# DMA queue in program order, and the two norms' statistics at other places, in a fused window-attention and Fourier kernel

## The chip, the core and the metric

The kernel runs on one core of one Trainium2 chip. The time is device microseconds (us) from the launch to the end of the program; the median of repeated runs is compared. A core has a matrix engine (TensorE, "PE" in the profile, with its weight loads as "PEld"), a vector engine (VectorE, "DVE"), an activation engine (ScalarE, "ACT"), a general engine (GpSimd, "POOL") and SyncE ("SP"), which here does nothing but issue DMA transfers. Each engine works through its own list of instructions in order; semaphores make one engine wait for another.

## What is computed

The input has 32 images of 56 x 56 pixels with 128 channels, float32. Layer 0 is a shifted-window attention, layer 1 a Fourier mixing with a feed-forward part; each has a group norm (32 groups of 4 channels) in front and a residual around it. Cut to what matters:

```python
def reference(x, ...):
    x = x + _L0_conv_ref(_gn(x), rpb_table, w_qkv, w_proj, b_proj)
    x = x + _L1_conv_ref(_gn(x), w0, w1, W1, b1, W2, b2)
    return x
# _gn: mean and variance of each group of 4 channels over the whole image
# _L0: roll by 3, cut into 7x7 windows, qkv, softmax(q k / sqrt(32) + bias + mask) v, projection
# _L1: DCT along the width, mix 32 modes with w0, inverse DCT; the same along the height with w1;
#      sum; then relu(h @ W1 + b1) @ W2 + b2
```

So layer 1's norm of an image can be finished only when the attention of all its rows is done, and layer 0's norm only when the whole image has been read.

## The kernel before: the parts that matter

An image is treated as 8 rows of windows (`NWR` = 8). The outer loop counts cycles: in cycle 8b + i the scores of row i of image b are made. A row's steps are spread over several cycles, so several rows are under way at once: three cycles later its values are multiplied and projected, and in the cycle after that its statistics for the second norm are taken. Layer 1 of image b follows 11 cycles behind: its stage c is cycle - 11 - 8b, and c goes from 0 to 15. Stage 0 of one image and stage 8 of the image before fall into the same cycle, the one in which row 3 of a later image has its scores.

The statistics of the second norm. `part` holds, for every row, the sums and the sums of squares; `fourier_stats` adds the 8 rows up, and a matmul with a constant matrix takes the mean over the partitions:

```python
def attn_sums(im, i):                      # one row, two halves
    nc.vector.tensor_reduce(im.part[:, 0, :, i], piece..., axis=AX.XY, op=ALU.add)
    yield
    nc.scalar.activation(sq, piece, AF.Square)
    nc.vector.tensor_reduce(im.part[:, 1, :, i], sq..., axis=AX.XY, op=ALU.add)
    yield

def fourier_stats(im):
    nc.vector.tensor_reduce(tot..., im.part..., axis=AX.X, op=ALU.add)
    yield
    pg = attn_bank()
    halved(pg[:, : C // 2], gmean, tot...)             # two matmuls, 64 output rows each
    ...                                                # own, ms, nm2, ve on VectorE
    nc.gpsimd.tensor_tensor(rstd, ve, mhalf, ALU.pow)  # the reciprocal root, on GpSimd
    nc.vector.scalar_tensor_tensor(out=shift, in0=ms[:, 0:1], scalar=-SQRT_S, in1=rstd, ...)
    yield
```

The first norm of the next image is a generator too. Its first part (on VectorE and GpSimd) ends with `rstd`; the second makes `nb` on VectorE and the scaled weights `im.w` on ScalarE; the third is a matmul of `nb`:

```python
def image_norm(im):
    yield
    nc.vector.bn_aggr(...); ...                        # eleven small VectorE steps
    nc.gpsimd.tensor_tensor(rstd, ve, mhalf, ALU.pow)
    yield
    nc.vector.scalar_tensor_tensor(out=nb, in0=gm, scalar=-1.0, in1=rstd, ...)
    nc.scalar.mul(im.w, wqkv, rstd)
    yield
    pb = attn_bank()
    halved(pb[:, 0:1], wqkv[:, 2 * C :], nb)
    ...
```

The feed-forward part reads the residual `res` back from DRAM (`scr`), adds a bias on GpSimd, and adds the result on VectorE when it is done:

```python
def ff_in(im, g):
    res = work.tile([P, 4, C], F32, tag="res", name="res")          # two buffers
    nc.sync.dma_start(res[:, :k], scr_tok[t0 : t0 + k * P]...)
    nc.gpsimd.tensor_tensor(res..., res..., b2sb..., ALU.add)
    ...                                                              # first matmul, relu -> hid
def ff_out(im, g):
    ...                                                              # second matmul -> pf
    nc.vector.tensor_tensor(res..., pf..., res..., ALU.add)
    nc.sync.dma_start(out_tok[...], res...)
```

One cycle of the steady part, with the order in which the instructions are written down:

```python
def halves_first(cycle, norm):
    last, j = row(cycle - 4)
    if last:
        sums = attn_sums(last, j); next(sums)      # sums of the row before
    im, i = row(cycle)
    if im: attn_qk(im, i, False)                   # q, k of this row
    next(norm)                                     # image_norm, first part
    if last: next(sums)                            # sums of squares
    for im, c in fourier(cycle):
        if c == 0: im.stats = fourier_stats(im); next(im.stats)      # tot
    for im, c in fourier(cycle):
        if c in FF_AT: ff_in(im, FF_AT.index(c))   # FF_AT = (8, 9, 10, 12, 13, 14, 15)
    for im, c in fourier(cycle):
        if c == 0: next(im.stats)                  # matmul of tot, rstd, shift

# then: values of row - 3, scores of this row, modes_back (inverse DCT, its sum into xf is
# VectorE's where it is along the width), transposes; and at the end of the cycle
def halves_last(cycle, norm):
    im, i = row(cycle)
    if im: attn_v(im, i, cycle)
    if has_ff(cycle): half_columns(cycle)          # the DCT (transform) or the mixing
    half_columns(cycle, True)
    load_back(cycle + 1); next_begin(cycle); load_first(cycle)       # DMA loads
    if row(cycle)[0]: attn_exp(cycle); attn_divide(cycle)
    next(norm)                                     # image_norm, second part
    im, j = row(cycle - 3)
    if im: last_out(cycle); attn_project(im, j)    # ff_out; projection, row stored to scr
    next(norm)                                     # image_norm, third part
```

`transform` and `modes_back` share four PSUM banks (`pc`). The order is kept as written on TensorE, ScalarE, VectorE and GpSimd; the order of the transfers on SyncE is left to the scheduler of the framework:

```python
with tc.manual_schedule(engines={ET.PE, ET.Activation, ET.DVE, ET.Pool}):
```

The first 11 cycles, before layer 1 starts, have their own routine (`first_rows`); there the statistics of the attention rows are taken four cycles behind in one go.

Of the kernel before, what the change touches and what calls it, by code (L numbers as in the profile page):

```python
# [17 lines left out]
C = 128  # L18
# [6 lines left out]
NWR = S // WS  # L25
# [23 lines left out]
def swin_fourier_kernel(  # L49
# [58 lines left out]
    def halved(dst, lhsT, rhs, start=True, stop=True):  # L108

        for p in range(0, dst.shape[0], P // 2):  # L110
            ps = slice(p, min(p + P // 2, dst.shape[0]))
            nc.tensor.matmul(dst[ps], lhsT=lhsT[:, ps], rhs=rhs, start=start, stop=stop)  # L112
# [19 lines left out]
    def const_load(shape, src, name):  # L132
        t = const.tile(shape, F32, tag=name, name=name)
        (nc.scalar if name in FIRST else nc.sync).dma_start(t, src)
        return t
# [47 lines left out]
    bm = const.tile([P, 2, 2, NP, 2, WT], F32, tag="bm", name="bm")  # L183
    nc.gpsimd.memset(bm, 0.0)
    rpb_f = rpb.rearrange("p (t u) y x -> p t u (y x)", u=2)
    for r in range(2):
        for t in range(2):
            for half in range(2):
                rows = slice(half * JP, half * JP + WT)
                for k, p0, p1 in ((0, 0, NP - half), (1, NP - half, NP)):  # L190
                    for p in range(p0, p1):
                        nc.vector.tensor_tensor(
                            bm[rows, r, t, p],
                            rpb_f[rows, t],
                            mask_sb[rows, r, k].unsqueeze(1).to_broadcast([WT, 2, WT]),
                            ALU.add,
                        )

    dct_w = const_load([TC, 2 * NM], dct, "dct_w")
    dct_h = const.tile([TC, 2 * NM], F32, tag="dct_h", name="dct_h")  # L200
    for r in range(0, TC, S):
# [375 lines left out]
    def fourier_stats(im):  # L577
        tot = small.tile([TC, 2, C // 4], F32, tag="tot", name="tot")
        nc.vector.tensor_reduce(
            tot.rearrange("p k g -> p (k g)"),  # L580
            im.part.rearrange("p k g i -> p (k g) i"),
            axis=AX.X,
            op=ALU.add,
        )
        yield
        pg = attn_bank()

        halved(pg[:, : C // 2], gmean, tot.rearrange("p k g -> p (k g)"))
        own = small.tile([P, 2, C // 4], F32, tag="own", name="own", bufs=1)
        nc.vector.scalar_tensor_tensor(  # L590
            out=own,
            in0=pg[:, : C // 2].rearrange("p (k g) -> p k g", k=2),
            scalar=4.0,
            in1=gavg.rearrange("p (g c) -> p g c", c=4)[:, :, 0]
            .unsqueeze(1)
            .to_broadcast([P, 2, C // 4]),
            op0=ALU.mult,
            op1=ALU.mult,
        )
        ms = small.tile([P, 2], F32, tag="ms", name="ms")  # L600
        nc.vector.tensor_reduce(ms, own, axis=AX.X, op=ALU.add)
        nm2 = small.tile([P, 1], F32, tag="nm2", name="nm2")
        nc.vector.scalar_tensor_tensor(
            out=nm2, in0=ms[:, 0:1], scalar=-1.0, in1=ms[:, 0:1], op0=ALU.mult, op1=ALU.mult
        )
        ve = small.tile([P, 1], F32, tag="ve1", name="ve1")
        nc.vector.scalar_tensor_tensor(
            out=ve, in0=nm2, scalar=1e-5, in1=ms[:, 1:2], op0=ALU.add, op1=ALU.add
        )
        rstd = small.tile([P, 1], F32, tag="rstd1", name="rstd1")  # L610
        nc.gpsimd.tensor_tensor(rstd, ve, mhalf, ALU.pow)
        shift = small.tile([P, 1], F32, tag="shift", name="shift")
        nc.vector.scalar_tensor_tensor(
            out=shift, in0=ms[:, 0:1], scalar=-SQRT_S, in1=rstd, op0=ALU.mult, op1=ALU.mult
        )
        im.rstd, im.shift = rstd, shift
        im.zT, im.zscr = {}, {}
        yield
# [197 lines left out]
    def row(r):  # L816
        return (images[r // NWR], r % NWR) if 0 <= r < NB * NWR else (None, 0)
# [12 lines left out]
    def load_back(cycle):  # L830
        for im, c in fourier(cycle):
            for width, g in back_groups(c):
                load_modes(im, width, g)

    def load_first(cycle):
        for im, c in fourier(cycle):
            if c == 0:
                load_columns(im, 0)
                load_columns(im, 1)

    def halves_first(cycle, norm):
        last, j = row(cycle - 4)
        if last:
            sums = attn_sums(last, j)
            next(sums)
        im, i = row(cycle)
        if im:
            attn_qk(im, i, False)
        next(norm)
        if last:  # L850
            next(sums)
        for im, c in fourier(cycle):
            if c == 0:
                im.stats = fourier_stats(im)
                im.cols = {}
                next(im.stats)
        for im, c in fourier(cycle):
            if c in FF_AT:
                ff_in(im, FF_AT.index(c))
        for im, c in fourier(cycle):  # L860
            if c == 0:
                next(im.stats)
# [46 lines left out]
    def next_groups(cycle):  # L909
        b, i = divmod(cycle, NWR)  # L910
        if b + 1 < NB:
            for j in {5: (0, 2), 6: (4, 6)}.get(i, ()):
                image_groups(images[b + 1], j)

    def last_out(cycle):
# [4 lines left out]
    def halves_last(cycle, norm):  # L920
        im, i = row(cycle)
        if im:
            attn_v(im, i, cycle)
        if has_ff(cycle):
            half_columns(cycle)
        half_columns(cycle, True)
        load_back(cycle + 1)
        next_begin(cycle)
        load_first(cycle)
        if row(cycle)[0]:  # L930
            attn_exp(cycle)
            attn_divide(cycle)
        next(norm)
        im, j = row(cycle - 3)
        if im:
            last_out(cycle)
            attn_project(im, j)
        next(norm)
# [10 lines left out]
    def first_rows(cycle, norm):  # L949
        im, i = row(cycle)  # L950
        if im:
            attn_qk(im, i, True)
        if cycle:
            attn_exp(cycle - 1)
        im3, i3 = row(cycle - 3)
        if im3:
            attn_values(im3, i3, cycle - 3)
        im2, i2 = row(cycle - 2)
        if im2:
            attn_transpose(im2, i2, cycle - 2)  # L960
        if cycle:
            attn_divide(cycle - 1)
        if im:
            attn_scores(im, i, cycle)
            attn_max(cycle)
        if im3:
            attn_project(im3, i3)
        next(norm)
        last, j = row(cycle - 4)
        if last:  # L970
            for _ in attn_sums(last, j):
                pass
        if im:
            attn_v(im, i, cycle)
        if cycle < NWR // 2:
            image_bias(im, 2 * cycle)
        next(norm)
        next_begin(cycle)
        next_groups(cycle)
        if cycle == CONV_BEGIN - 1:  # L980
            attn_exp(cycle)
            attn_divide(cycle)
            last, j = row(cycle - 1)
            attn_transpose(last, j, cycle - 1)
        next(norm)

    def nothing():
        while True:
            yield

    ET = mybir.EngineType
    with tc.manual_schedule(engines={ET.PE, ET.Activation, ET.DVE, ET.Pool}):
        images[0] = image_begin(0)
        for i in range(0, NWR, 2):
            image_groups(images[0], i)
        for _ in image_norm(images[0]):
            pass
        norm = nothing()
        for cycle in range(NB * NWR + CONV_BEGIN + FF_AT[-1] - NWR + 1):
            if cycle < CONV_BEGIN:  # L1000
                first_rows(cycle, norm)
            else:
                halves_first(cycle, norm)
                if not row(cycle - 3)[0]:
                    half_columns(cycle)
                    half_columns(cycle, True)
                    load_first(cycle)
                    last_out(cycle)
                    quarters(cycle)
                    load_back(cycle + 1)  # L1010
                    continue
                if not has_ff(cycle):
                    half_columns(cycle)
                eighths(cycle)
                quarters(cycle)
                if row(cycle)[0] and cycle % 2:
                    attn_max(cycle)
                full(cycle)
                halves_last(cycle, norm)
            b, i = divmod(cycle, NWR)  # L1020
            norm = nothing()
            if i == NWR - 2 and b + 1 < NB:
                norm = image_norm(images[b + 1])
                next(norm)

# [61 lines left out]
```

## Time and profile before

Three runs took 3663.43, 3664.92 and 3668.95 us; the median is 3664.92. The profiled run spans 3662.0 us.

| engine | busy, us | share of the span | instructions |
|---|---|---|---|
| PE | 3574.7 | 98% | 72064 |
| PEld | 2832.1 | 77% | 72064 |
| DVE | 2216.2 | 61% | 4738 |
| ACT | 2147.2 | 59% | 4044 |
| POOL | 1368.1 | 37% | 1421 |

How to read it: an engine's busy time is the union of its instructions; what is left of the span is idle time, and the profile says for each idle stretch what ended it ("PE ... <- DVE nb" is time in which PE waited for the instruction on DVE that writes `nb`). A busy PE need not be at its peak: the ends of matmuls are modelled, and the clock may be halved. By stretches of 100 us, PE is busy 73.20 us in the first, 81.88 in the second, 96.47 in the third and 97.69 to 99.81 from then on to 3600 us; the mean granted clock is 0.95 in the first stretch, 0.90 in the second and 1.00 after it. The matmul of `tot` comes once per image: at 2222.8 us and at 3117.4 us, eight images apart, so an image takes 111.8 us. The DMA engines are busy for some 40% of the span.

### The profile page before, as it was taken

How to read it: one execution, taken by the hardware profiler on the slowest of the kernel's cores; microseconds unless marked ns; L12 is line 12 of the kernel's file. 1: busy time of each engine (PE TensorE's matmuls, PEld its weight loads, DVE VectorE, ACT ScalarE, POOL GpSimd, SP SyncE). 2: the span in 40 equal slices, each digit the busy share in tenths (PEclk: the TensorE clock that was granted, in tenths of full speed). 3: DMA queues.
4: the chain of work that ended last, by engine and by line, in shares of the span. 5: the costliest groups of instructions: out<-in, count | busy, mean ns of one | idle time of the engine just before them, and what ended most of it. 6: DMA issues, size and time to landing. Idle time of an engine off the chain costs nothing.

```text
span 3662.0 us, 161441 instructions
## 1 busy us (share of the span) xinstructions
PE 3574.7 (98%) x72064; PEld 2832.1 (77%) x72064; DVE 2216.2 (61%) x4738; ACT 2147.2 (59%) x4044; POOL 1368.1 (37%) x1421
## 2 busy tenths in 40 slices
PE   7899999999999999999999999999999999999999
PEld 5677777777787777787877877777778778777776
DVE  7666665666666666656666666666566666666641
ACT  5555566555556555566555566555655556565553
POOL 5333334333434333333334343334433343433321
PEclk9999999999999999999999999999999999999999
DMA  4333433444334444334443344443344433443343
GB/s 114 85 101 105 117 97 108 108 108 113 107 96 113 110 111 109 99 105 109 111 113 105 99 109 113 105 113 100 106 109 111 113 106 98 109 113 105 97 117 98
DMA packets 687349, 390.29 MB, mean 107 GB/s; under 512 B 39967, under 2 KB 657600, under 8 KB 686400
## 3 DMA queue, kind: packets, MB, share of 16 engines
q1 hardware_dynamic: 686045, 379.65, 38.1%
q8 instruction: 567, 9.29, 1.1%
q14 instruction: 126, 1.03, 0.1%
q10 hardware_dynamic: 611, 0.32, 0.0%
HBM read 218.29 MB, written 161.48 MB: 104 GB/s over the span
## 4 chain that ended last, share of the span: by engine, by line
PE 77%; DVE 15%; ACT 3%; POOL 3%; issue 2%; DMA 1%; SPq 0%; POOLq 0%; DVEq 0%; ACTq 0%
PE pc L112 30%; PE pa L112 12%; PE pc L640 6%; PE pa L406 5%; PE pc L674 5%; PE pa L428 5%; PE pa L472 5%; PE pa L497 4%; PE pc L713 3%; PE pa L273 3%; POOL a L447 2%; DVE sm L458 2%; DVE a L436 2%; DVE xf L724 2%; ACT a L453 2%
## 5 line engine op out<-in xcount | busy, mean ns | idle before, releaser
L447 POOL TENSOR_TENSOR a<-a,mx 128x784 f32<-128x784 f32 x256 | 389.3, 1521 | 1439.7 <-DVE mx L446 1247.8
L112 PE MATMUL pc<-wff,hid 128*64 128x128 f32 x12544 | 739.9, 273 | 1.3 <-ACT hid L758 1.0
L112 PE MATMUL pc<-xf,wff 128*64 128x512 f32 (+2 forms) x3584 | 718.4, 539 | 1.0 <-DVE xf L724 1.0
L112 PEld LDWEIGHTS pc<-wff,hid 128*64 128x64 f32 x12544 | 702.7, 137 | 7.4 <-ACT hid L758 4.6
L458 DVE TENSOR_REDUCE sm<-a 128x16 f32<-128x784 f32 x256 | 248.2, 970 | 693.8 <-ACT a L453 692.9
L461 POOL TENSOR_TENSOR a<-a,rs 128x784 f32<-128x784 f32 x256 | 389.0, 1520 | 568.8 <-DVE rs L460 491.0
L758 ACT ACTIVATE hid<-pc,b1sb 128x512 f32<-128x512 f32 (+2 forms) x896 | 526.7, 632 | 76.3 <-PE pc L112 74.2
L112 PEld LDWEIGHTS pc<-xf,wff 128*64 128x64 f32 x3584 | 286.6, 137 | 361.1 <-issue 257.5
L377 ACT ACTIVATE q<-pa,bqkv 128x392 f32<-128x392 f32 x256 | 150.4, 588 | 466.7 <-PE pa L112 460.9
L112 PE MATMUL pa<-xw,wn 128*64 128x392 f32 (+1 forms) x2048 | 393.3, 499 | 3.2 <-DVE a L436 3.2
L528 DVE TENSOR_SCALAR oT<-pa,bqkv 128x98 f32<-128x98 f32 (+2 forms) x768 | 171.1, 278 | 271.1 <-PE pa L497 271.1
L746 POOL TENSOR_TENSOR res<-res,b2sb 128x512 f32<-128x512 f32 (+2 forms) x256 | 264.0, 1037 | 113.6 <-DMA res<-scr 113.6
L453 ACT ACTIVATE a<-a 128x784 f32<-128x784 f32 x256 | 222.4, 869 | 112.2 <-POOL a L447 111.8
L413 ACT COPY v<-pa 128x512 f32<-128x512 f32 x256 | 150.9, 589 | 232.2 <-PE pa L406 232.2
L304 POOL TENSOR_TENSOR xl<-xl,bproj 112x512 f32<-112x512 f32 (+1 forms) x256 | 286.8, 1142 | 0.0
L406 PE MATMUL pa<-wn,xw 128*64 128x128 f32 x4096 | 283.1, 280 | 3.1 <-issue 3.1
L497 PEld LDWEIGHTS pa<-aT,v 49*32 49x32 f32 x16384 | 172.6, 105 | 139.6 <-issue 120.1
L436 DVE TENSOR_TENSOR a<-pa,bm 128x392 f32<-128x392 f32 x512 | 264.9, 560 | 24.1 <-PE pa L428 0.5
L480 ACT COPY aT<-pa 113x452 f32<-113x452 f32 x256 | 139.5, 545 | 206.1 <-PE pa L472 202.2
L406 PEld LDWEIGHTS pa<-wn,xw 128*64 128x64 f32 x4096 | 220.9, 137 | 37.7 <-issue 8.9
L394 DVE TENSOR_SCALAR k<-pa,heads,bqkv 128x392 f32<-128x392 f32 x245 | 167.2, 683 | 135.7 <-ACT k L386 133.1
L782 DVE TENSOR_TENSOR res<-pc,res 128x512 f32<-128x512 f32 (+3 forms) x257 | 140.2, 556 | 180.3 <-PE pc L112 146.5
(89 smaller groups left out, 5748.3 us busy)
## 6 DMA issues: line engine op xcount, KB each, us to landing
zscr<-z SPq DMA_DIRECT2D x512, 112.0 KB
htok<-scr SPq DMA_DIRECT2D x256, 196.0 KB
zT<-zscr SPq DMA_DIRECT2D x192, 256.0 KB
res<-scr SPq DMA_DIRECT2D x160, 256.0 KB
out_dram<-res SPq DMA_DIRECT2D x160, 256.0 KB
scr<-xl SPq DMA_DIRECT2D x128, 224.0 KB
xl<-in_x_dram SPq DMA_DIRECT2D x32, 784.0 KB
xl<-in_x_dram SPq DMA_DIRECT2D x32, 672.0 KB
```

The source lines that it names most:

```text
L112: nc.tensor.matmul(dst[ps], lhsT=lhsT[:, ps], rhs=rhs, start=start, stop=stop)
L304: nc.gpsimd.tensor_tensor(piece, piece, bproj.unsqueeze(1).to_broadcast([TC, e - a, C]), ALU.add)
L406: nc.tensor.matmul(pv[hs, j * C : (j + 1) * C], lhsT=im.xw[i][:, w * WT : w * WT + JP], rhs=im.w[:, 2 * C : 3 * C], start=True, stop=True,)
L436: nc.vector.tensor_tensor(a[:, 2 * hp : 2 * hp + 2, :, 0:WT].rearrange("p u w j -> p w u j"), ps[hp][:, :RT].rearrange("p (w u j) -> p w u ...
L447: nc.gpsimd.tensor_tensor(a3, a3, mx.unsqueeze(2).to_broadcast([P, 2 * NWR, WT]), ALU.subtract)
L453: nc.scalar.activation(a3, a3, AF.Exp)
L458: nc.vector.tensor_reduce(sm, a3, axis=AX.X, op=ALU.add)
L461: nc.gpsimd.tensor_tensor(a3, a3, rs.unsqueeze(2).to_broadcast([P, 2 * NWR, WT]), ALU.mult)
L497: nc.tensor.matmul(po4[u][h * HD : (h + 1) * HD, 2 * f + e], lhsT=v[ks, 2 * f + e, h * HD : (h + 1) * HD], rhs=im.aT[i][f][ks, h, e * JP : ...
L640: nc.tensor.matmul(py[hs, c * 2 * NM : (c + 1) * 2 * NM], lhsT=tok[:, c, hs], rhs=dct_sb, start=True, stop=True,)
L746: nc.gpsimd.tensor_tensor(res[:m, c0:c1], res[:m, c0:c1], b2sb[:m].unsqueeze(1).to_broadcast([m, c1 - c0, C]), ALU.add,)
L758: nc.scalar.activation(hf[:, :n], ph[:, :n], AF.Relu, bias=b1sb[:, f : f + 1])
```

## The change

It has five parts.

1. SyncE joins the engines whose order is kept as written, so that the DMA queue is filled in program order instead of the scheduler's.
2. The statistics of the second norm: the sum over rows (`tot`) is taken ahead of the last row, over 7 rows, at the start of the cycle; the last row's sums are added by a second matmul that accumulates into the same PSUM bank. At the first image the last row's sums are moved to the end of the cycle before.
3. The second part of the first norm (`nb` and the scaled weights) is put ahead of the exponential and the division instead of behind them.
4. The bias-and-mask table for the last row of an image (16 of 32 VectorE instructions) is made in cycle 1 instead of at the start.
5. Image 1's windows are cut and its norm is made one cycle earlier.

The idea of the parts 2 to 5 is to take VectorE and ScalarE work out of the way of matmuls that wait for it; part 1 makes the order of the transfers predictable.

```diff
@@ tables @@
-    for r in range(2):
+    def bias_and_mask(r):
         for t in range(2):
             for half in range(2):
... (the same 16 VectorE additions for each r)
+    bias_and_mask(0)
@@ fourier_stats @@
-            im.part.rearrange("p k g i -> p (k g) i"),
+            im.part.rearrange("p k g i -> p (k g) i")[:, :, : NWR - 1],
...
-        halved(pg[:, : C // 2], gmean, tot.rearrange("p k g -> p (k g)"))
+        rows = (tot, im.part[:, :, :, NWR - 1])
+        for k, t in enumerate(rows):
+            t = t.rearrange("p k g -> p (k g)")
+            halved(pg[:, : C // 2], gmean, t, start=(k == 0), stop=(k == 1))
@@ halves_first @@
-        last, j = row(cycle - 4)
-        if last:
-            sums = attn_sums(last, j)
-            next(sums)
-        im, i = row(cycle)
-        if im:
-            attn_qk(im, i, False)
-        next(norm)
-        if last:
-            next(sums)
         for im, c in fourier(cycle):
             if c == 0:
                 im.stats = fourier_stats(im)
                 im.cols = {}
                 next(im.stats)
+        last, j = row(cycle - 4)
+        sums = attn_sums(last, j) if last and cycle > CONV_BEGIN else nothing()
+        next(sums)
+        im, i = row(cycle)
+        if im:
+            attn_qk(im, i, False)
+        next(norm)
+        next(sums)
@@ next_groups @@
-            for j in {5: (0, 2), 6: (4, 6)}.get(i, ()):
+            for j in {(4 if b == 0 else 5): (0, 2), (5 if b == 0 else 6): (4, 6)}.get(i, ()):
@@ halves_last @@
+        next(norm)
         if row(cycle)[0]:
             attn_exp(cycle)
             attn_divide(cycle)
-        next(norm)
@@ first_rows @@
+        if cycle == 1:
+            bias_and_mask(1)
...
         if cycle == CONV_BEGIN - 1:
             attn_exp(cycle)
             attn_divide(cycle)
+            for _ in attn_sums(im3, i3):
+                pass
@@ main loop @@
-    with tc.manual_schedule(engines={ET.PE, ET.Activation, ET.DVE, ET.Pool}):
+    with tc.manual_schedule(engines={ET.PE, ET.Activation, ET.DVE, ET.Pool, ET.SP}):
...
-            if i == NWR - 2 and b + 1 < NB:
+            if i == (NWR - 2 if b else NWR - 3) and b + 1 < NB:
                 norm = image_norm(images[b + 1])
                 next(norm)
```

More of the change, by code (lines that the diff above doesn't have):

```diff
@@ L833, in load_back, with nothing @@
                 load_modes(im, width, g)
+    def nothing():
+        while True:
+            yield
     def load_first(cycle):
@@ L985, in first_rows @@
         next(norm)
-    def nothing():
-        while True:
-            yield
     ET = mybir.EngineType
-    with tc.manual_schedule(engines={ET.PE, ET.Activation, ET.DVE, ET.Pool}):
+    with tc.manual_schedule(engines={ET.PE, ET.Activation, ET.DVE, ET.Pool, ET.SP}):
         images[0] = image_begin(0)
```

## The prediction

> **What bounds the kernel now.** I read the page's first part, then the waits of PE, then the timeline where PE waits.
>
> ```profile
> PE 3574.7 (98%) x72064; PEld 2832.1 (77%) x72064; DVE 2216.2 (61%) x4738; ACT 2147.2 (59%) x4044; POOL 1368.1 (37%) x1421
> ```
>
> PE is idle for 3662.0 - 3574.7 = 87 us in all, so no rearrangement of the other engines can bring much more than that. By stretches of 100 us, 27 + 18 us of it lie in the first 200 us, about 1 us per 100 us after that, and 6 us at the end. The waits of PE (engine, line, what it waited for: total, times, longest):
>
> ```profile
> PE pa L112 <- DVE nb L357: 18.5, 22, 5.0
> PE pa L112 <- DVE tot L579: 18.1, 26, 4.8
> ...
> PE pa L112 <- DVE a L436: 3.2, 1, 3.2
> ```
>
> These three are what parts 2 to 4 of the change aim at. The timeline of PE shows how they are spread (start, duration, engine, line, instruction; idle time before it in brackets):
>
> ```profile
> 82.54 0.28 PE L112 MATMUL pa<-nb,wqkv 128*64 128x1 f32 x4 [4.90 <-DVE nb L357]
> 110.97 0.48 PE L112 MATMUL pa<-tot,gmean 112*64 112x64 f32 x4 [4.76 <-DVE tot L579]
> 167.08 0.38 PE L112 MATMUL pa<-nb,wqkv 128*64 128x1 f32 x4 [5.03 <-DVE nb L357]
> 167.28 2.90 PE L112 MATMUL pa<-xw,wn 128*64 128x393 f32 x8
> 206.10 0.34 PE L112 MATMUL pa<-tot,gmean 112*64 112x64 f32 x4 [2.00 <-DVE tot L579]
> ```
>
> Big waits occur only in the filling phase. In the steady part it is 0.45 us for `tot` and 0.16 us for `nb` per image. The line at 167.28 shows a second cost of a long wait: eight matmuls that take 1.49 us elsewhere take 2.90 us, because the clock is halved (0.50 in the stretch 165 to 170 us).
>
> The cycle in which `tot` is used, for one steady image:
>
> ```profile
> 2220.69 0.38 SPq L551 DMA_DIRECT2D scr<-xl  x1
> 2220.78 1.27 POOL L746 TENSOR_TENSOR res<-res,b2sb 128x512 f32<-128x512 f32 x1
> 2221.87 0.38 SPq L739 DMA_DIRECT2D res<-scr  x1
> ...
> 2224.18 0.55 POOL L611 TENSOR_TENSOR rstd<-ve,mhalf 128x1 f32<-128x1 f32 x1 [2.12 <-DVE ve L607]
> 2224.76 0.16 DVE L613 SCALAR_TENSOR_TENSOR shift<-ms,rstd 128x1 f32<-128x1 f32 x1 [0.66 <-POOL rstd L611]
> ...
> 2226.37 1.74 DVE L724 TENSOR_TENSOR xf<-pc,xf 128x448 f32<-128x448 f32 x4
> ...
> 2227.03 3.06 PEld L640 LDWEIGHTS pc<-dct_w,xl 112*64 112x64 f32 x102 [0.37 <-DVE xf L724]
> ```
>
> The reader is to see two things. The `res` added on POOL at 2220.78 was fetched a cycle earlier: the fetch at 2221.87 is already the next group's, since the scheduler's order runs one group ahead. And `rstd` on POOL, `shift` on DVE, the rest of DVE's list and the transform on PE (L640, which needs a PSUM bank that `xf` empties) form a chain without slack: in the waits, PEld of L640 waits for `xf` 23 times, 8.6 us in total.
>
> [...] the granted clock is 0.50 in 30 to 35 us and 165 to 170 us, after waits of 3.2 and 5.0 us. [...] `rstd` comes after the `res` addition in every steady image, as written. This carries the prediction. [...] So the 0.38 us of a `res` issue is not its cost; I take that from the tail, where POOL waits for it:
>
> ```profile
> 3637.93 0.36 SPq L739 DMA_DIRECT2D res<-scr  x1
> 3640.80 1.27 POOL L746 TENSOR_TENSOR res<-res,b2sb 128x512 f32<-128x512 f32 x1 [6.00 <-DMA res<-scr]
> ```
>
> That is 2.87 us from issue to use (2.8 to 3.8 at other 256 KB groups of the tail).
>
> **The change part by part.** The changed instruction lists show that each engine keeps its instructions, bar 32 more matmul calls of two halves each.
>
> *Statistics (part 2), steady.* DVE now does `tot` (0.69 us for 8 rows, so 0.61 for 7, an estimate by elements) right behind the projection's addition, then the sums, `k`, and the squares. It works through these back to back, so the last result is ready hardly sooner: what it saves is 0.08 us of `tot` and two pauses of about 0.1 us after dependent neighbours, 0.2 to 0.3 us. PE can run the first matmul pair while it waits, so the added pair (0.27 us) is hidden. Worth 0.2 us an image, not 0.45, and only if nothing later holds the image up.
>
> *First norm (part 3), steady.* `nb` no longer waits for the sum and reciprocal; ScalarE has 1.24 us of idle time ahead of the exponential, in which the 0.60 us of scaled weights fit. 0.16 us x 29 is at most 4.6; I count -3.5 us.
>
> *First norm, filling.* At 167 us `nb` (166.82) can come right after the maximum, at about 163.1. PE starts 4 us earlier; `k` then holds it up for about 1.4 us; part of the half-speed stretch goes. -3.5 us.
>
> *Mask (part 4).* 32 additions take 5.69 us in all; half of them, 2.8 us, leave the start, where PE waited 3.17 us for `a`. They return in cycle 1 and delay DVE by about 0.6 us. -2.2 us.
>
> *First image's statistics and image 1's norm (parts 2 and 5).* At 111 us DVE is busy without a pause until `tot`; moving sums within that stretch gains about 0.7 us. Image 1's norm keeps the same neighbours one cycle earlier, DVE being just as far behind there (it starts the projection's addition at 69.56 where PE is through at 69.42): its 4.9 us move, they don't go. I count -0.5 together, with 0.2 us taken off for the first image's columns, which now queue behind an image load.
>
> *DMA order (part 1).* `res` of a group is now issued in its own cycle, behind the store of the row before. At the image above that is at 2220.69 + 0.38 = 2221.07. With 2.87 us plus some queueing behind that store I take 3.1 us: the POOL addition starts at 2224.17 and ends at 2225.44. `rstd` stands behind it, so it starts 1.26 us later than now (2224.18); `shift`, `a`, `xf` and the transform follow, as they have no slack. 1.1 to 1.3 us an image, in 31 cycles where one image's statistics meet another's feed-forward. A few images have slack from other pauses of PE, so 1.1 x 31 = +34 us. The 0.2 us of part 2 are lost in this. The other cycles have room: POOL idles 4 to 7 us before it next has work. Image loads and columns swap places, but columns still have about 5 us left.
>
> Sum: 34 - 3.5 - 3.5 - 2.2 - 0.5 = +24 us, so 3665 + 24 = 3689 us; I say 3687.
>
> **The rivals.** (a) *The DMA order is hidden.* For it: POOL is busy 37% and PE hardly ever waits for a DMA. Against it: the slack in that one cycle is zero. Then only the gains stay, with part 2's 0.2 x 29: about -15 us, 3650 us. (b) *All named waits vanish*, with their half-speed stretches: 18.5 + 18.1 + 3.2 + about 6 = -46 us, 3619 us. Against it: DVE has no pause ahead of `tot`, and image 1's norm isn't shortened. (c) *The transfers queue longer*, 3.8 us: 0.7 us more an image, 3709 us, more if waits of 2 us begin to halve the clock.
>
> **Range and chances.** I put about 70% on the new POOL wait, 25% on (a), the rest on (b) and (c) beyond their sizes. The range 3644 to 3713 holds all but the extremes. 2% is 73 us: faster by that would need nearly all of PE's idle time, slower would need 2.4 us more an image. Faster 0.01, within 2% 0.96, slower 0.03.
>
> **What would show it.** Right: POOL's `res` addition waits for a DMA some 31 times in the steady part, `rstd` starts 1.0 to 1.5 us later after the matmul of `tot` than now, and PE has a wait of about 1 us ahead of L640 for `xf` once an image; the image period grows from 111.8 to about 112.8 us. PE's waits for `nb` fall to one of about 5 us (image 1) plus remnants, and that for `a` at 28 us nearly goes. Wrong: if `res` lands before `ve` is made, or if DVE gets other work done ahead of `shift`, the period falls to about 111.5 us.

## The result, and the profile after

The changed kernel takes 3696.12 us (median of four runs, 3693.26 to 3698.84). The kernel before, run on the same chip, takes 3666.93 us (3663.43 to 3669.57). The ratio is 1.008, with a 95% interval of 1.0063 to 1.0098: 29 us slower, where the working came to 24.

The first part of the page, as it was read before (busy time, share of the span, instructions):

```profile
PE 3581.4 (97%) x72192; PEld 2831.5 (77%) x72192; DVE 2212.9 (60%) x4738; ACT 2148.8 (58%) x4044; POOL 1374.4 (37%) x1421
```

The span is 3697.1 us, so PE's idle time grew from 3662.0 - 3574.7 = 87 us to 3697.1 - 3581.4 = 116 us: of the 35 us by which the span grew, 28 are idle time of PE, and 7 are busy time. The waits of PE (what it waited for: total us, times, longest) say where it lies (`htok` holds the columns of an image, read back for the DCT along the height):

```profile
PE pc L645 <- DVE xf L729: 53.3, 29, 3.0
PE pa L112 <- DVE nb L359: 10.3, 3, 4.7
...
PE pc L645 <- DMA htok<-scr: 4.9, 1, 4.9
PE pa L112 <- DVE tot L581: 4.0, 1, 4.0
...
PE pa L112 <- DVE a L438: 1.3, 1, 1.3
```

Three of the waits that the change aimed at shrank: `nb` from 18.5 us in 22 waits to 10.3 in 3, `tot` from 18.1 us in 26 waits to a single one of 4.0, and `a` from 3.2 to 1.3. The first line took their place: 29 waits for `xf` ahead of the transform (L645; L640 before), one an image, 1.84 us each. The next view is the timeline of one steady image in the cycle in which the statistics are used (start, duration, engine, line, instruction; idle time before it in brackets):

```profile
2240.99 0.36 SPq L553 DMA_DIRECT2D scr<-xl  x1
2241.40 0.49 SPq L744 DMA_DIRECT2D res<-scr  x1
...
2242.49 0.29 PE L112 MATMUL pa<-tot,gmean 112*64 112x64 f32 x4
...
2243.93 0.16 DVE L612 SCALAR_TENSOR_TENSOR ve<-nm,ms 128x1 f32<-128x1 f32 x1
...
2244.56 1.28 POOL L751 TENSOR_TENSOR res<-res,b2sb 128x512 f32<-128x512 f32 x1 [3.43 <-DMA res<-scr]
...
2245.79 0.55 POOL L616 TENSOR_TENSOR rstd<-ve,mhalf 128x1 f32<-128x1 f32 x1
2246.37 0.16 DVE L618 SCALAR_TENSOR_TENSOR shift<-ms,rstd 128x1 f32<-128x1 f32 x1 [2.28 <-POOL rstd L616]
...
2247.97 1.74 DVE L729 TENSOR_TENSOR xf<-pc,xf 128x448 f32<-128x448 f32 x4
...
2248.64 3.48 PE L645 MATMUL pc<-dct_w,xl 112*64 112x64 f32 x112 [1.76 <-DVE xf L729]
```

Read it from below. The transform waits 1.76 us for `xf`, `xf` stands behind `shift`, and `shift` waits 2.28 us for `rstd`. But `ve`, the operand of `rstd`, is ready at 2243.93 + 0.16 = 2244.09. What holds `rstd` is its place in GpSimd's list, behind the `res` addition, and that addition waits for a transfer issued at 2241.40. The wait of GpSimd that matters is one of many. After:

```profile
POOL res L751 <- DMA res<-scr: 941.8, 189, 10.9
```

And before:

```profile
POOL res L746 <- DMA res<-scr: 113.6, 16, 12.0
```

Of the 256 additions 189 now wait, against 16, and 941.8 us of waiting is far more than was lost. Only the wait that has a statistics instruction behind it, once an image, is on the path.

To see cycle by cycle what moved, I take the starts of the first query/key matmul of each cycle on PE's timeline; the distance between two is the length of a cycle. Medians over 28 steady images, means in brackets where they differ much:

| kernel | cycle with `tot` (row 3), us | cycle with the first norm (row 7), us |
|---|---|---|
| before | 17.08 (17.30) | 13.70 |
| after | 18.39 (18.87) | 13.33 |
| after, DMA order by the scheduler | 16.75 (16.89) | 13.33 |
| before, DMA in program order | 18.34 (18.42) | 13.70 |
| before, first norm moved (part 3) | 17.06 (17.28) | 13.33 |
| before, statistics (part 2) | 16.75 (16.84) | 13.71 |

The medians of the other six cycles agree within 0.05 us in all six kernels. So the steady part is two numbers, and the rows from the third on belong to the experiments below.

### The profile page after: what moved, and what is told of

Read it like the earlier page. It is cut to its first block, busy times and chain, and to the rows that moved or that the text cites. A ratio compares the mean times of both kernels' runs of the same rounds, so it can differ in the third digit from the quotient of the medians.

```text
span 3697.1 us, 161637 instructions
## 1 busy us (share of the span) xinstructions
PE 3581.4 (97%) x72192; PEld 2831.5 (77%) x72192; DVE 2212.9 (60%) x4738; ACT 2148.8 (58%) x4044; POOL 1374.4 (37%) x1421
## 5 line engine op out<-in xcount | busy, mean ns | idle before, releaser
L751 POOL TENSOR_TENSOR res<-res,b2sb 128x512 f32<-128x512 f32 (+2 forms) x256 | 264.6, 1039 | 998.8 <-DMA res<-scr 941.8
L112 PEld LDWEIGHTS pc<-xf,wff 128*64 128x64 f32 x3584 | 273.1, 137 | 374.0 <-issue 270.5
L448 DVE TENSOR_REDUCE mx<-a 128x16 f32<-128x784 f32 x256 | 246.3, 962 | 4.3
L112 PE MATMUL pa<-wproj,oT 128*64 128x128 f32 (+1 forms) x3584 | 246.4, 274 | 1.8 <-DVE oT L530 1.8
```

Of the source, the lines that this page charges most:

```text
L448: nc.vector.tensor_reduce(mx, a3, axis=AX.X, op=ALU.max)
L751: nc.gpsimd.tensor_tensor(res[:m, c0:c1], res[:m, c0:c1], b2sb[:m].unsqueeze(1).to_broadcast([m, c1 - c0, C]), ALU.add,)
```

## The experiments

My theory: the order of the DMA queue alone makes the loss, through the `res` addition ahead of `rstd`; the other parts gain. Rivals: the other parts bring nothing or lose; or other transfers in the new order (the first image's columns, the image loads) cost the time. The first four kernels shared the runs of the kernel before (3664.29 us).

**Program order off, parts 2 to 5 kept.**

```diff
-    with tc.manual_schedule(engines={ET.PE, ET.Activation, ET.DVE, ET.Pool, ET.SP}):
+    with tc.manual_schedule(engines={ET.PE, ET.Activation, ET.DVE, ET.Pool}):
```

> The changed kernel with the DMA queue left to the scheduler again (part 1 undone, parts 2 to 5 kept). Theory A, the order of the DMA queue is the whole loss, by way of the residual addition that now stands ahead of rstd on GpSimd: 53 us of TensorE's waits for xf, some 12 us of half-speed stretches behind them and about 6 us at the first image's columns go, so 3620 to 3645 us, below the kernel before. Theory B, the statistics' new places cost something of their own (a busier VectorE ahead of the values and scores): 3665 us or more.

Measured: 3634.53 us, ratio 0.992 (0.9907 to 0.9934). The other parts are worth about 30 us. Among the larger waits of PE neither `xf` nor `htok` is left:

```profile
PE pa L112 <- DVE nb L359: 10.3, 3, 4.7
...
PE pc L718 <- issue: 5.8, 8, 1.1
...
PE pa L112 <- DVE tot L581: 4.0, 1, 4.0
```

**Program order alone, on the kernel before.** The same line of code, the other way round.

> The kernel before with only the DMA queue put in program order (part 1 alone). Theory A: rstd starts about 1.3 us later in 31 cycles, 40 us, with a few half-speed stretches and about 6 us at the first image's columns: 3705 to 3730 us. Theory B: within 10 us of the kernel before, 3657 to 3677 us.

Measured: 3700.57 us, ratio 1.0099 (1.0085 to 1.0113), so +36 us, a little less than expected. Its waits of PE:

```profile
PE pc L640 <- DVE xf L724: 38.1, 30, 1.8
...
PE pa L112 <- DVE nb L357: 19.5, 32, 5.0
PE pa L112 <- DVE tot L579: 19.0, 29, 4.8
...
PE pc L640 <- DMA htok<-scr: 4.8, 1, 4.8
```

The wait for `xf` is there without any other part of the change, 1.27 us an image, beside the old waits for `nb` and `tot`. The two runs together show the order as the cause of the loss. They also show that the parts don't add: 36 us for the order alone, but 29.2 + 29.8 = 59 us when it is put on top of parts 2 to 5 (the change is 29.2 us above the kernel before of its own runs, parts 2 to 5 without it 29.8 us below that of theirs). That difference is taken up below.

**Which transfer it is.** In the next kernel the order stays, and only the GpSimd addition is taken out of `ff_in` and written behind `rstd`. If the loss comes from `rstd` standing behind it, it must go.

```diff
@@ ff_in: the GpSimd addition becomes ff_bias @@
@@ halves_first @@
     for im, c in fourier(cycle):
         if c == 0: next(im.stats)                  # matmul of tot, rstd, shift
+    for im, c in fourier(cycle):
+        if c in FF_AT: ff_bias(im, FF_AT.index(c))
```

> The changed kernel with all five parts, the DMA queue in program order, but GpSimd's addition to the residual written behind rstd instead of ahead of it; the transfers are the same and land at the same time. Theory A: the waits of TensorE for xf ahead of the transform shrink from 53 us to under 12 us, 3625 to 3645 us. Rival C, it is the transfers' later landing or their crowding and not GpSimd's order: 3685 us or more, with the same waits.

Measured: 3657.37 us, ratio 0.9984 (0.9976 to 0.9991). That is 6.9 us below the kernel before, where the change is 29.2 above it, so most of the loss is gone. But it is outside the range expected, and 23 us worse than with the scheduler's order. Two of the waits in this kernel:

```profile
POOL res L763 <- DMA res<-scr: 854.3, 165, 11.3
...
PE pc L645 <- DVE xf L729: 24.2, 23, 1.2
```

GpSimd still waits for `res` 165 times; with `rstd` no longer behind them, these waits cost little. PE still waits for `xf`, up to 1.2 us an image. `rstd` came early now, so something else held `xf`. The timeline of this kernel:

```profile
2324.82 0.55 POOL L616 TENSOR_TENSOR rstd<-ve,mhalf 128x1 f32<-128x1 f32 x1 [3.05 <-DVE ve L612]
...
2325.33 1.28 POOL L763 TENSOR_TENSOR res<-res,b2sb 128x512 f32<-128x512 f32 x1
2325.40 1.23 DVE L618 SCALAR_TENSOR_TENSOR shift<-ms,rstd 128x1 f32<-128x1 f32 x1 [0.66 <-POOL rstd L616]
...
2328.74 3.43 PE L645 MATMUL pc<-dct_w,xl 112*64 112x64 f32 x110 [1.22 <-DVE xf L729]
```

`shift` is one element per partition, and it takes 1.23 us instead of 0.16. It begins 0.07 us after GpSimd's addition and ends with it. Where it happened to begin first, in another image of the same run, it was short:

```profile
2214.38 0.16 DVE L618 SCALAR_TENSOR_TENSOR shift<-ms,rstd 128x1 f32<-128x1 f32 x1 [0.66 <-POOL rstd L616]
2214.43 1.28 POOL L763 TENSOR_TENSOR res<-res,b2sb 128x512 f32<-128x512 f32 x1
```

Over all 32 images, `shift` is long in 23, and in each of these the addition began 0.07 us ahead of it. In the other nine it took 0.16 us, and there PE waited for the transform 0.16 us at most. So the part that was left had a second cause, one that my own experiment brought in: the addition right behind `rstd` runs just when VectorE wants `shift`.

**The columns ahead of the next image's load**, on top of that kernel, for the first image's wait for `htok`.

```diff
         load_back(cycle + 1)
-        next_begin(cycle)
         load_first(cycle)
+        next_begin(cycle)
```

> As the run with the addition behind rstd, and the loads of the columns issued ahead of the load of the next image's first half. Theory A: the wait of 4.9 us at the first image's columns, and its half-speed stretch, go: 4 to 7 us less than that run, 3620 to 3640 us. Rival: the wait is for the store of the last row and not for the image load ahead in the queue, then no difference (within 2 us).

Measured: 3655.37 us, ratio 0.9978 (0.9969 to 0.9987). The wait for `htok` (4.9 us in the change, 4.1 us in the kernel that this one builds on) is gone from the waits of PE, but the medians differ by 2 us, not by 4 to 7, and the intervals overlap: the loss is not in the columns.

If the picture is right, two quite different kernels must reach the time of the scheduler's order: one with the addition further behind, one with the fetch earlier. With them ran parts 3 and 2 on the kernel before (its time in these runs: 3664.41 us).

**The addition behind the whole row's work**, after the maximum has been subtracted on GpSimd.

```diff
@@ halves_first and the tail: ff_bias called later @@
     full(cycle)
+    add_bias(cycle)          # ff_bias for the groups of this cycle
```

> The changed kernel, DMA queue in program order, with GpSimd's addition to the residual written behind the subtraction of the row maxima, well away from rstd and shift. In the run with the addition just behind rstd, shift took 1.22 us instead of 0.16 in most images, with the addition starting 0.07 us ahead of it. Theory D, VectorE and GpSimd collide there: shift takes 0.16 us in all images, TensorE's wait for xf goes, and the time is that of the run with the scheduler's order plus about 5 us at the first image's columns: 3636 to 3646 us. Rival C, later landing transfers cost something by themselves: 3652 us or more.

Measured: 3633.72 us, ratio 0.9917 (0.9903 to 0.9931). The cycle with `tot` takes 16.75 us, as with the scheduler's order, and program order is kept. The 5 us that I had added for the first image's columns did not show: there is still a wait of 3.1 us, and the time is that of the scheduler's order. The larger waits of PE have no `xf`:

```profile
PE pa L112 <- DVE nb L359: 10.3, 3, 4.7
...
PE pa L112 <- DVE tot L581: 4.0, 1, 4.0
PE pc L645 <- DMA htok<-scr: 3.3, 2, 3.1
```

The durations of `shift` (least, median, greatest ns) are the other half of the evidence. With the addition right behind `rstd`:

```profile
L618 DVE SCALAR_TENSOR_TENSOR shift<-ms,rstd x32: 158/1220/1229, 114.8 to 3542.0; 128x1 f32<-128x1 f32 x32
```

With the addition behind the maximum, where one of the 32 is still long:

```profile
L618 DVE SCALAR_TENSOR_TENSOR shift<-ms,rstd x32: 158/159/1222, 113.3 to 3517.7; 128x1 f32<-128x1 f32 x32
```

**The fetch one cycle ahead**, with the addition left where the change has it and the columns first.

```diff
@@ ff_in: the two loads of res become ff_fetch @@
@@ halves_first, behind ff_in @@
+    for im, c in fourier(cycle):
+        if c + 1 in FF_AT: ff_fetch(im, FF_AT.index(c + 1))
```

> The changed kernel, DMA queue in program order and GpSimd's addition where the change has it, but the residual's fetch written one cycle earlier (as the scheduler's order had it), and the columns' loads ahead of the image load. Theory A: the addition finds its data, rstd is on time: 3628 to 3640 us, like the run with the scheduler's order. Rival: program order costs in other places too (zT, columns, image loads): 3650 us or more.

Measured: 3632.64 us, ratio 0.9913 (0.9899 to 0.9927). Here the addition still stands ahead of `rstd`, exactly as in the change; only its data comes a cycle earlier. The whole loss is gone, and GpSimd's waits for `res` are as few as before:

```profile
POOL res L757 <- DMA res<-scr: 113.5, 16, 15.5
```

It was the landing of `res`, and not the addition's 1.28 us as such. The columns' place can't account for it: with the addition behind `rstd` it made 2 us.

**The first norm ahead of the division, alone** (part 3, on the kernel before).

```diff
+        next(norm)
         if row(cycle)[0]:
             attn_exp(cycle)
             attn_divide(cycle)
-        next(norm)
```

> The kernel before with part 3 alone (second part of the first norm ahead of exponential and division), scheduler's DMA order. By the prediction's working, 3.5 us in the steady part and 3.5 us in the filling: 3655 to 3660 us. By the cycle lengths read from the traces since (13.70 us before, 13.33 us after in the cycle with the norm), 0.37 us x 29 + 3.5 us: 3647 to 3653 us.

Measured: 3649.93 us, ratio 0.9961 (0.9948 to 0.9975), so -14.5 us, as the cycle lengths say and twice what the prediction's working said.

**The statistics alone** (part 2 with the first image's earlier sums, on the kernel before): the diff is that of `fourier_stats`, `halves_first` and the sums in `first_rows` in the change, without the rest.

> The kernel before with part 2 alone (tot ahead of the last row, accumulating matmul, first image's sums a cycle earlier), scheduler's DMA order. By the prediction's working 0.2 us x 29 + 0.7 us: 3656 to 3660 us. By the cycle lengths read since (17.08 us before, 16.75 us with the scheduler's order and all other parts), 0.33 us x 29 + 0.7 us: 3651 to 3656 us.

Measured: 3651.15 us, ratio 0.9965 (0.9953 to 0.9978), so -13.3 us, again at what the cycle lengths say. The two together make 27.7 of the 29.8 us that all of parts 2 to 5 bring under the scheduler's order.

**What is best, and what parts 4 and 5 are worth.** The last three ran together (kernel before: 3666.72 us). The first is the addition behind the maximum with the columns first; the others take that kernel and undo one thing.

```diff
@@ image 1's windows and norm back @@
-            for j in {(4 if b == 0 else 5): (0, 2), (5 if b == 0 else 6): (4, 6)}.get(i, ()):
+            for j in {5: (0, 2), 6: (4, 6)}.get(i, ()):
...
-            if i == (NWR - 2 if b else NWR - 3) and b + 1 < NB:
+            if i == NWR - 2 and b + 1 < NB:
@@ mask back: the whole table at the start @@
     bias_and_mask(0)
+    bias_and_mask(1)
...
-        if cycle == 1: bias_and_mask(1)
```

> All five parts, DMA queue in program order, GpSimd's addition behind the subtraction of the maxima, and the columns' loads ahead of the image load (the wait of 3.1 us for the first image's columns was still there in the run with the addition moved). Expected 3 to 5 us below that run: 3628 to 3632 us. If the two runs are the same, the first image's columns wait for something else behind which the image load doesn't count.

Measured: 3638.28 us, ratio 0.9923 (0.9909 to 0.9936). I had expected the columns to bring some 3 us, and they brought nothing that can be told from zero. The filling did get faster: the `tot` matmul of image 1 comes at 199.58 us instead of 201.63. But from there on it is slower: from image 2's `tot` matmul to the last image's it took 3208.4 us instead of 3201.2. That is one execution of each. The fastest images take 110.7 us in both, but of the 28 full images in this stretch 7 take more than 111.0 us in the first and 15 here. What these pauses are stays open.

> As the best version, with part 5 undone for image 1 (its windows and norm one cycle later, as in the kernel before). The prediction said that the wait moves and doesn't go: within 2 us of the best version. If the change's intent holds, 3 us or more slower.

Measured: 3638.40 us, ratio 0.9924 (0.9912 to 0.9936): moving image 1's norm does nothing here, as expected.

> As the best version, with part 4 undone (the whole table of bias and mask made at the start). The prediction said 2.2 us: 1 to 4 us slower than the best version. Rival: what is saved at the start comes back in cycle 1, within 1 us.

Measured: 3637.13 us, ratio 0.9919 (0.9906 to 0.9933): nor does the table made in cycle 1. The 1 to 4 us expected for it did not show; the rival, that the saving comes back, fits.

No kernel beats the two repairs at 3633 us, and these don't differ from each other or from the scheduler's order by more than their intervals.

## Why the prediction was right, and which terms were off

**The DMA order: the mechanism as told, the size short in company.** The image shown above gives each term. From the issue of `res` to its use: 2244.56 - 2241.40 = 3.16 us, where 3.1 was taken. The wait of PE ahead of the transform in the kernel with the order alone: 1.27 us, where 1.1 to 1.3 was taken; 36.3 us in all, where +34 was. `rstd`, however, came 3.30 us after the matmul of `tot` (2245.79 - 2242.49) against 1.36 us before (2224.18 - 2222.82). That is 1.94 us later, not 1.0 to 1.5: the matmul of `tot` itself now starts earlier, 1.50 us behind the issue of the row's store instead of 2.13, and the end is fixed by the transfer. This is the matmul in the kernel before, in the image that the prediction shows:

```profile
2222.82 0.34 PE L112 MATMUL pa<-tot,gmean 112*64 112x64 f32 x4 [0.45 <-DVE tot L579]
```

An image, by the sum of its eight cycles, takes 112.6 us (median of 28, mean 113.0) where 112.8 was said, and GpSimd's new waits and the wait for `xf` are where they were said to be.

**Part 2's gain "lost behind the order": right, but mis-sized.** Worth 0.2 us an image by the working, it is worth 17.08 - 16.75 = 0.33 us. In the changed kernel it shows as a longer wait for `xf` (1.84 instead of 1.27 us) and not as a shorter cycle. PE is ready sooner for a transform that can't start sooner.

**What the working left out: half-speed stretches behind the longer waits.** It stood only as an aside of rival (c), waits of 2 us that begin to halve the clock. The timeline of PE in the changed kernel has both kinds of image:

```profile
550.66 3.49 PE L645 MATMUL pc<-dct_w,xl 112*64 112x64 f32 x112 [1.71 <-DVE xf L729]
...
664.18 6.24 PE L645 MATMUL pc<-dct_w,xl 112*64 112x64 f32 x112 [2.98 <-DVE xf L729]
```

The same 112 matmuls take 6.24 us behind a wait of 2.98 us, and the mean granted clock is 0.55 from 664 to 671 us, against 1.00 from 550 to 555 us. In six steady images the transform takes 4.9 to 6.2 us instead of 3.49, about 10 us in all, and its wait in these is 2.15 to 2.98 us; no shorter wait in the steady part of this kernel has such a stretch behind it. But the length of this wait alone doesn't decide. Of the nine waits of 2.10 us and more three were followed by full speed, one of 2.82 us among them (granted clock 1.00 from 1122 to 1125 us), and with the order alone one of 1.84 us by a transform of 5.03 us, the only such one in its steady part:

```profile
1121.92 3.48 PE L645 MATMUL pc<-dct_w,xl 112*64 112x64 f32 x112 [2.82 <-DVE xf L729]
```

```profile
3037.03 5.03 PE L640 MATMUL pc<-dct_w,xl 112*64 112x64 f32 x112 [1.84 <-DVE xf L724]
```

The prediction had seen a clock of 0.50 after waits of 3.2 and 5.0 us; in the six images of the change and the one with the order alone the waits were 1.84 to 2.98 us, and what decides besides the wait is not shown. The mean granted clock is 0.992 in the profile of the change and 0.995 in that with the order alone; the change's other runs have 0.993 to 0.995, so the 10 us are those of the profiled execution. This and part 2's swallowed gain account for most of what the order costs beyond its own 36 us: in the means of the cycle with `tot`, (17.30 - 16.89) x 28 = 11 us for part 2, plus 10 us, out of 59.0 - 36.3 = 23.

**Part 3, steady: mis-sized by half.** 0.16 us an image was read from PE's waits for `nb`. The cycle became 0.37 us shorter, and the whole part is worth 14.5 us, not 7.0. The step that failed is to take the idle time shown for the delay. This is one image in the kernel before:

```profile
1953.79 0.82 PE L112 MATMUL pa<-wproj,oT 128*64 128x128 f32 x12
1954.77 0.28 PE L112 MATMUL pa<-nb,wqkv 128*64 128x1 f32 x4 [0.16 <-DVE nb L357]
```

And the same image with part 3 alone:

```profile
1945.21 0.82 PE L112 MATMUL pa<-wproj,oT 128*64 128x128 f32 x12
1945.87 0.23 PE L112 MATMUL pa<-nb,wqkv 128*64 128x1 f32 x4
```

From the projection's start to that of the `nb` matmul it is 0.98 us before and 0.66 after, 0.32 us less, though the idle time shown is 0.16. Where nothing waits, the second row begins 0.16 us ahead of the modelled end of the first (0.82 - 0.66), so the idle time shown leaves that much out.

**Part 3, filling: right.** The `nb` wait of 5.03 us at 167 us is 1.16 us now, as the second line below shows; about 3.5 us were counted. From the timeline of PE in the changed kernel:

```profile
77.45 0.38 PE L112 MATMUL pa<-nb,wqkv 128*64 128x1 f32 x4 [4.42 <-DVE nb L359]
...
112.10 0.48 PE L112 MATMUL pa<-tot,gmean 112*64 112x64 f32 x4 [3.98 <-DVE tot L581]
...
127.65 3.25 PE L645 MATMUL pc<-dct_h,htok 112*64 112x64 f32 x56 [4.90 <-DMA htok<-scr]
...
167.57 0.28 PE L112 MATMUL pa<-nb,wqkv 128*64 128x1 f32 x4 [1.16 <-DVE nb L359]
```

**The first image's columns: the step that failed in the filling.** 0.2 us was taken off for them; the third line shows a wait of 4.90 us and a mixing that then takes 3.25 us at a granted clock of 0.50 (1.80 us where the wait is gone). So the filling gained 1.1 us by the start of image 1's statistics (204.98 against 206.10, the `tot` matmul's start), not the 6.2 of the sum's terms for the filling (3.5 + 2.2 + 0.5). "Columns still have about 5 us left" held for the other images: it was read in the steady part, and the first image was not looked at by itself. Removing this wait alone brought little in the end (the columns-first runs), so it is a miss in the sum of the filling more than in the total.

**Mask and image 1's norm.** The norm's wait moved and didn't go, as said: 4.42 us at 77 us, for 4.90 at 82. The wait for `a` fell from 3.17 to 1.31 us, but a new one of 1.96 us for `aT` came behind it, and the -2.2 us counted for the mask are not to be found in a time.

**Rival (a), the order hidden, would have been** the kernel with the scheduler's order: 3634.53 us, where the working made it 3650, half the gain. That the total came out near is partly luck, two errors against each other. The sum had 9.7 us of gains, and parts 2 to 5 bring 29.8; it had 34 us of loss, and in their company the order costs 59, the wait for the first image's columns included.

## What to carry to other kernels

When a queue's order changes, look at each consumer that stands, in its engine's list, in front of a short instruction on the path: a transfer that the engine could wait for at leisure becomes a wait of everything behind it (here 3.43 us for `res`, and a `rstd` that came 1.94 us later). Either issue the load a cycle earlier or write its consumer where nothing urgent follows; both gave back the whole loss here (3633 and 3634 us, against 3634.53 with the scheduler's order). And gains ahead of an event whose moment is fixed elsewhere become longer waits (here 1.84 us for `xf` instead of 1.27), so price the parts of a change together and not each against the old kernel.

## What the runs showed of the hardware that was not expected

A VectorE instruction of one element per partition, `shift`, took 1.22 us instead of 0.16 us in 23 of 32 images of the kernel with the addition right behind `rstd`; in each of them GpSimd had begun a 1.28 us addition 0.07 us before it. With that addition behind the maximum it was long in one image of 32, and the median was 0.159 us. In the image at 2214.38 us, shown above, it began 0.05 us ahead of the addition, and it took 0.16 us. What holds it up inside the chip is not shown; the trace shows when it ends, which is with the addition (2326.63 against 2326.61 us in the image at 2325.40 us). There it took nearly as long as GpSimd's instruction beside it, 1.23 us of 1.28, and PE then waited 1.22 us for `xf`.
